# Mixing and transposing softmax heads with two 64x128 TensorE tiles in place of four 64x64 tiles

## The chip, the cores and the metric

The kernel runs on one core of a Trainium2 chip. A core has five engines with instruction streams of their own: TensorE (PE, matrix multiply, results to PSUM), VectorE (DVE), ScalarE (ACT), GpSimd (POOL) and SyncE (SP, which starts DMAs here). The profile shows TensorE in two rows: PE for the matmuls, PEld for the loads of their stationary operand ("weight loads"), which can run beside matmuls. The metric is the device time of one execution in microseconds (us); lower is better. All data is 32-bit floating point.

TensorE multiplies a stationary operand, held in an array of 128 rows by 128 columns, by a moving operand that is streamed past it. A matmul smaller than the array can be put on a part of it, a tile; where its operands lie in the partitions of SBUF and its result in those of PSUM says which tile. A 64x64 tile takes 64 rows (the summed dimension) and 64 columns (the partitions of the result), and four of them fill the array. A 64x128 tile takes 64 rows and all columns, and two fill the array.

## The reference

Four sequences of 2048 tokens with 256 features run through a layer of attention with 16 heads of width 16, whose heads are mixed before and after the softmax, and then through a soft mixture of experts. Both have a residual sum and a layer norm. What matters here is the attention:

```python
logits = jnp.einsum('bhid,bhjd->bhij', q, k) * SCALE
logits = jnp.einsum('bhij,gh->bgij', logits, Wpre)
attn = jax.nn.softmax(logits, axis=-1)
attn = jnp.einsum('bhij,gh->bgij', attn, Wpost)
out = jnp.einsum('bhij,bhjd->bhid', attn, v)
```

For every query i and key j there are 16 scores, which are mixed across heads by Wpre, put through a softmax over keys, mixed across heads by Wpost, and used to weight the values.

## The kernel before

Per sequence, three stages follow one another: `qkv` (projections, rotary embedding, transposes), `attention`, and `moe`. The attention takes over nine tenths of the time. It works on pairs of query blocks: a block is 8 queries with 16 heads, which together fill 128 partitions, and a pair n has two blocks x = 0, 1. A sequence has 128 pairs, all four have 512. The 2048 keys are split into two halves j of 1024 (`HALF`).

For each pair and each half of the keys these steps are run, by functions inside `attention`:

- `raw_bank` (matmul L368, copy L375): scores of the 16 queries and heads for 512 keys, four banks k per half, each on four 128x32 tiles. VectorE or ScalarE copies each bank from PSUM to SBUF as `raw`.
- `logits` (L389): mixing by Wpre, on 64x64 tiles, into PSUM tiles `l` of pool `ps_l`.
- `top` (L402, VectorE): the negated maximum of each row. `expo` (L410, ScalarE): the exponential, to SBUF as `e`, with row sums.
- `weights` (L421 to L432, mostly GpSimd): once per pair, the block matrix `w` in which Wpost is multiplied by the softmax's factors.
- `mix` (matmul L461, copy L470): the changed step. It multiplies by Wpost and transposes at the same time: the stationary operand is a piece of `e` (64 rows of queries and heads, some keys as columns), the moving operand is the matching 64 rows of `w` (64 columns: 16 mixed heads by 4 queries). The result has keys on its partitions, as the next step needs it.
- `values` (L485): the product with v, twice per two pairs, on four 128x32 tiles, 64 columns each.

A call of `mix` is for one block x and one half j. It takes two PSUM tiles `pts[r]`, one for the upper and one for the lower 64 partitions of `e`, each with eight key tiles a (`HT`) of 128 keys. For each a and each r it issued two matmuls, c = 0 and 1, of 64 keys each. So a call has 8 x 2 x 2 = 32 matmuls, and each is recorded in the trace as two weight loads and two matmul instructions, as is every 32-bit matmul here that is not a transpose: 64 of each per call, 128 per two calls, and 131072 in all. Then each `pts[r]` is copied to `aT` by VectorE (V) or ScalarE (S_).

The PSUM tiles of `raw_bank`, `mix` and `values` all come from pool `ps_t`, which has four buffers (L72). A call of `mix` holds two of them until its copies are done; so two calls in a row hold all four, and the raw bank after them starts when the first copy has given one back.

The loop over n is a software pipeline: scores of pair n+1, logits and exponentials of pair n, mixing of pair n-1, values of earlier pairs. On PE the order in a pair, as the trace has it, is: logits of the first half, four raw banks, `mix` of block 0 for both halves (first burst, 128 instructions); logits of the second half, `mix` of block 1 for both halves (second burst, 128 instructions), four raw banks, values. In the source the second half's calls stand so:

```python
if prv:
    mix(n - 1, 1, 0, (S_, S_))
if cur:
    top(n, j, 0)
    expo(n, j, 0)
if prv:
    mix(n - 1, 1, 1, (V, S_))
```

The framework orders the instructions of each engine, so an engine's order may differ from the source's: in the trace, ScalarE runs this exponential before the two copies of the call that stands ahead of it.

Of the kernel before, what the change touches and what calls it, by code (L numbers as in the profile page):

```python
# [16 lines left out]
P = 128  # L17
# [8 lines left out]
def kernel(  # L26
# [20 lines left out]
    nc = tc.nc  # L47
# [36 lines left out]
    for r in range(P // HC):  # L84
        c, i = divmod(r % (KC * IQ), IQ)
# [248 lines left out]
    def attention(b, y, qT, kT, v):  # L334
# [107 lines left out]
        def mix(n, x, j, engs):  # L442

            s = state[n]
            grp, k = divmod(2 * n + x, NB)
            if k == 0 and j == 0:
                aT[grp] = work.tile([P, NT, HEADS, GI], F32, tag="aT", name=f"aT_{b}_{grp}")  # L450
            pts = [
                ps_t.tile([P, HT, HEADS * IQ], F32, tag="t", name=f"t_{b}_{n}_{x}_{j}_{r}")
                for r in range(2)
            ]
            e = s["e", x, j]
            for a in range(HT):
                for r in range(2):
                    rows = slice(64 * r, 64 * (r + 1))
                    for c in range(2):
                        k0 = a * P + 64 * c  # L460
                        nc.tensor.matmul(  # L461
                            pts[r][64 * c : 64 * (c + 1), a, :],
                            e[rows, k0 : k0 + 64],
                            s["w"][rows, 2 * x + j, :],
                            start=True,
                            stop=True,
                        )
            for r in range(2):
                i0 = k * IB + r * IQ
                engs[r](  # L470
                    aT[grp][:, ts(j, HT), :, i0 : i0 + IQ],
                    pts[r].rearrange("p a (g i) -> p a g i", i=IQ),
                )
# [47 lines left out]
        for n in range(n_pairs + 3):  # L521
# [4 lines left out]
            for j in range(2):  # L526
# [4 lines left out]
                if j == 0:  # L531
# [15 lines left out]
                    if prv:  # L547
                        mix(n - 1, 0, 0, (V, S_))
                        mix(n - 1, 0, 1, (V, S_))
                else:  # L550
                    if prv:
                        mix(n - 1, 1, 0, (S_, S_))
# [207 lines left out]
```

## Time and profile before

| | us |
|---|---|
| median of 3 runs | 10240.56 (10240.32 to 10242.80) |
| the profiled execution | 10242.24 |
| its span, first to last instruction | 10240.5 |
| PE busy, all matmuls | 9268.5 |
| PE busy with raw scores (L368) | 3739.1 |
| PE busy with mixing (L461) | 2183.9 |
| PE busy with logits (L389) | 2070.1 |
| PE busy with values (L485) | 1018.0 |
| copies of mixed tiles (L470), ACT and DVE | 1450.4 and 1058.2 |

Busy time of PE counts a moment once, however many tiles work in it, so several matmuls side by side are no longer than one. In a group's line, the first figure after the bar is busy time in us and the second the mean duration of one instruction in ns; that mean is from issue to last result and is far longer than the spacing of instructions, since they overlap. "128*32", "64*64" and so on before the shapes are the rows and columns of the array that an instruction uses. The mean granted clock of TensorE over the execution is 0.986 of the full one; in the attention stage it is 1.00.

### The profile page before, as it was taken

The numbers are of one execution on the slowest core, as the hardware profiler recorded it, in microseconds if no ns is written. First come the engines' busy times: TensorE is split into PE (matmuls) and PEld (weight loads), VectorE is DVE, ScalarE is ACT, GpSimd is POOL, SyncE is SP. The second block draws the span as 40 slices with busy tenths as digits, with TensorE's granted clock in tenths as the row PEclk, the third lists the DMA queues.
The fourth block names the chain that finished last, engine by engine and source line by source line (L and its number), as shares of the span: only waits on it lengthen the run. The fifth ranks groups of instructions, "written<-read, shape, count | busy, mean of one in ns | idle before, by whom it ended". The sixth has DMA issues, their size and how long they took to land.

```text
span 10240.5 us, 523545 instructions
## 1 busy us (share of the span) xinstructions
PE 9268.5 (91%) x248404; PEld 5008.8 (49%) x248404; DVE 5613.3 (55%) x9064; ACT 4995.1 (49%) x9766; POOL 1284.9 (13%) x3409
## 2 busy tenths in 40 slices
PE   8999999997899999999689999999968999999996
PEld 4445545444444445445444545444544444444454
DVE  5555555554555555555455555555545555555554
ACT  3555555553455555555345555555534555555553
POOL 2111111111211111111121111111112111111111
PEclk9999999998999999999899999999989999999998
DMA  0000000000000000000000000000000000000000
GB/s 23 5 5 5 4 5 5 5 4 17 19 5 5 5 4 5 5 5 4 17 19 5 5 5 4 5 5 5 4 17 18 5 5 5 4 5 5 4 4 18
DMA packets 63584, 74.04 MB, mean 7 GB/s; under 512 B 30080, under 2 KB 59904, under 8 KB 61440
## 3 DMA queue, kind: packets, MB, share of 16 engines
q8 instruction: 1946, 31.88, 1.3%
q1 hardware_dynamic: 26880, 25.18, 0.8%
q10 hardware_dynamic: 34560, 15.36, 0.6%
q14 instruction: 198, 1.62, 0.1%
HBM read 32.13 MB, written 8.39 MB: 4 GB/s over the span
## 4 chain that ended last, share of the span: by engine, by line
PE 80%; ACT 9%; DVE 8%; issue 2%; POOL 1%; ACTq 0%; DMA 0%; POOLq 0%; DVEq 0%
PE s L368 36%; PE l L389 19%; PE t L461 10%; PE o L485 9%; DVE m L402 6%; ACT e L410 5%; ACT aT L470 3%; PE pqk L289 1%; PE pz L509 1%; PE pf L680 1%; PE l_d L197 1%; PE o_d L236 1%; POOL xn L591 0%; PE pv L294 0%; POOL xn L592 0%
## 5 line engine op out<-in xcount | busy, mean ns | idle before, releaser
L368 PE MATMUL s<-kT,qb 128*32 128x512 f32 x32768 | 3739.1, 596 | 551.4 <-ACT aT L470 551.3
L402 DVE TENSOR_REDUCE m<-l 128x1 f32<-128x1024 f32 x2048 | 2412.7, 1220 | 1269.8 <-PE l L389 1269.8
L410 ACT ACTIVATE e<-l,m 128x1024 f32<-128x1024 f32 x2048 | 2285.8, 1121 | 1262.7 <-DVE m L402 1262.6
L375 ACT COPY raw<-s 128x512 f32<-128x512 f32 x2048 | 1211.7, 592 | 2809.0 <-PE s L368 2808.4
L461 PEld LDWEIGHTS t<-w,e 64*64 64x64 f32 x131072 | 2103.4, 135 | 754.0 <-issue 685.9
L368 PEld LDWEIGHTS s<-kT,qb 128*32 128x32 f32 x32768 | 966.7, 109 | 2886.8 <-issue 1797.2
L461 PE MATMUL t<-w,e 64*64 64x64 f32 x131072 | 2183.9, 219 | 43.0 <-issue 34.9
L389 PE MATMUL l<-raw,wmix_sb 64*64 64x512 f32 x16384 | 2070.1, 596 | 7.2 <-ACT e L410 3.6
L470 ACT COPY aT<-t 128x512 f32<-128x512 f32 x2560 | 1450.4, 589 | 396.2 <-PE t L461 395.8
L375 DVE COPY raw<-s 128x512 f32<-128x512 f32 x2048 | 1354.7, 681 | 350.3 <-PE s L368 349.6
L470 DVE COPY aT<-t 128x512 f32<-128x512 f32 x1536 | 1058.2, 689 | 338.2 <-PE t L461 338.0
L485 PEld LDWEIGHTS o<-aT,v 128*32 128x32 f32 x65536 | 997.0, 110 | 329.3 <-issue 176.8
L485 PE MATMUL o<-aT,v 128*32 128x64 f32 x65536 | 1018.0, 220 | 31.6 <-issue 26.5
L423 POOL TENSOR_TENSOR f<-m,m 128x4 f32<-128x4 f32 x512 | 101.6, 198 | 6568.8 <-DVE m L421 6568.8
L389 PEld LDWEIGHTS l<-raw,wmix_sb 64*64 64x64 f32 x16384 | 566.5, 133 | 679.6 <-issue 616.8
L429 DVE RECIPROCAL z<-z 128x2 f32<-128x2 f32 x512 | 85.1, 166 | 1081.5 <-POOL z L428 1081.5
L496 DVE COPY aoT<-o 128x32 f32<-128x32 f32 x512 | 98.1, 192 | 1005.9 <-PE o L485 1005.7
L410 ACT ACTIVATION_READ_ACCUMULATOR e<-l,m 128x1 f32 x2048 | 421.9, 206 | 0.0
L343 POOL TENSOR_TENSOR qb<-qT,hmask 128x256 f32<-128x256 f32 x512 | 313.6, 634 | 73.3 <-PE s L368 73.3
L432 POOL TENSOR_TENSOR w<-wblk_sb,f 128x256 f32<-128x256 f32 x512 | 313.7, 613 | 40.3 <-POOL f L430 0.5
L426 POOL TENSOR_TENSOR zf<-f,z 128x4 f32<-128x4 f32 x512 | 102.5, 200 | 987.2 <-ACT f L424 987.2
L315 POOL TENSOR_TENSOR s<-qk,wq 128x256 f32<-128x256 f32 x128 | 115.9, 924 | 478.4 <-DVE qk L299 478.4
(123 smaller groups left out, 2602.0 us busy)
## 6 DMA issues: line engine op xcount, KB each, us to landing
x<-in_x_dram SPq DMA_DIRECT2D x64, 128.0 KB
xr<-in_x_dram SPq DMA_DIRECT2D x64, 128.0 KB
out_dram<-y SPq DMA_DIRECT2D x16, 512.0 KB
wm<-in_w_dram ACTq DMA_DIRECT2D x8, 512.0 KB
wm<-in_w_dram ACTq DMA_DIRECT2D x4, 1024.0 KB
wq<-in_wqkvT_dram ACTq DMA_DIRECT2D x4, 768.0 KB
wq<-in_bqkv_dram ACTq DMA_DIRECT2D x4, 384.0 KB
wq<-in_rope_dram ACTq DMA_DIRECT2D x4, 256.0 KB
```

What stands on the lines that cost most here:

```text
L315: nc.gpsimd.tensor_mul(s[:, :, a, :], qk[:, :, 1 - a, :], ss[a])
L343: nc.gpsimd.tensor_tensor(qb, qT[:, :, ts(n, 2 * IB)].unsqueeze(3).to_broadcast([P, KC, 2 * IB, HC]), hmask.unsqueeze(1).unsqueeze(1).to_b ...
L368: nc.tensor.matmul(pr[32 * c : 32 * (c + 1), :], qb[:, c % 2, i0 : i0 + IQ, :].rearrange("p i h -> p (i h)"), kT[:, c % 2, j0 : j0 + 512], ...
L375: eng(raws[n][j, u][:, ts(jj, 512)], pr)
L389: nc.tensor.matmul(pls[x][64 * u : 64 * (u + 1), n0 : n0 + 512], wmix_sb[64 * x : 64 * (x + 1), :], raws[n][j, u][64 * x : 64 * (x + 1), n ...
L402: nc.vector.tensor_reduce(s["m2"][:, x, j : j + 1], s["l", j][x], AX.X, ALU.max, negate=True)
L410: nc.scalar.activation(e, s["l", j][x], AF.Exp, bias=s["m2"][:, x, j : j + 1], accum_out=s["z2"][:, x, j : j + 1],)
L426: nc.gpsimd.tensor_tensor(zf, f, z2, ALU.mult)
L432: nc.gpsimd.tensor_tensor(w, wblk_sb.rearrange("p g i -> p (g i)").unsqueeze(1).to_broadcast([P, 4, HEADS * IQ]), f.rearrange("p x j -> p ...
L461: nc.tensor.matmul(pts[r][64 * c : 64 * (c + 1), a, :], e[rows, k0 : k0 + 64], s["w"][rows, 2 * x + j, :], start=True, stop=True,)
L470: engs[r](aT[grp][:, ts(j, HT), :, i0 : i0 + IQ], pts[r].rearrange("p a (g i) -> p a g i", i=IQ),)
L485: nc.tensor.matmul(po[32 * c : 32 * (c + 1)].rearrange("p a i -> p (a i)"), v[:, t, g0 * HD : (g0 + 2) * HD], at[:, t, g0 : g0 + 2, :].rea ...
```

## The change

Inside `mix`, the loop over the two halves c of a key tile is gone. One matmul takes all 128 keys of a key tile as columns of its stationary operand, and writes all 128 partitions of the PSUM tile. A call has 16 matmuls on two 64x128 tiles of the array (upper and lower rows), in place of 32 on four 64x64 tiles. What is multiplied, the moving operand, the PSUM tiles and the copies out of them stay as they were.

```diff
             for a in range(HT):
                 for r in range(2):
                     rows = slice(64 * r, 64 * (r + 1))
-                    for c in range(2):
-                        k0 = a * P + 64 * c
-                        nc.tensor.matmul(
-                            pts[r][64 * c : 64 * (c + 1), a, :],
-                            e[rows, k0 : k0 + 64],
-                            s["w"][rows, 2 * x + j, :],
-                            start=True,
-                            stop=True,
-                        )
+                    nc.tensor.matmul(
+                        pts[r][:, a, :],
+                        e[rows, ts(a, P)],
+                        s["w"][rows, 2 * x + j, :],
+                        start=True,
+                        stop=True,
+                    )
```

## The prediction

> **What bounds the kernel now.** I read the page's busy shares first, then the chain that ended last, then the waits, then the timeline of one pair of query blocks in mid-kernel.
>
> ```profile
> PE 9268.5 (91%) x248404; PEld 5008.8 (49%) x248404; DVE 5613.3 (55%) x9064; ACT 4995.1 (49%) x9766; POOL 1284.9 (13%) x3409
> ...
> PE 80%; ACT 9%; DVE 8%; issue 2%; POOL 1%; ACTq 0%; DMA 0%; POOLq 0%; DVEq 0%
> ...
> L461 PEld LDWEIGHTS t<-w,e 64*64 64x64 f32 x131072 | 2103.4, 135 | 754.0 <-issue 685.9
> L368 PEld LDWEIGHTS s<-kT,qb 128*32 128x32 f32 x32768 | 966.7, 109 | 2886.8 <-issue 1797.2
> L461 PE MATMUL t<-w,e 64*64 64x64 f32 x131072 | 2183.9, 219 | 43.0 <-issue 34.9
> ```
>
> TensorE is the bound: busy 91% of the span, 80% of the chain. The mixing matmul (L461) is 2184 us of it. Of the rest, one wait matters, shown by the waits of PE (us in total, times, longest):
>
> ```profile
> PE s L368 <- ACT aT L470: 551.3, 492, 1.5
> ```
>
> Once in nearly each of the 512 pairs, the next raw-score bank waits until ScalarE has copied a mixed tile out of PSUM. The timeline of PE, and then that of ACT, show where:
>
> ```profile
> 4012.73 2.10 PE L461 MATMUL t<-w,e 64*64 64x64 f32 x128
> 4014.64 1.90 PE L389 MATMUL l<-raw,wmix_sb 64*64 64x512 f32 x16
> 4016.36 2.04 PE L461 MATMUL t<-w,e 64*64 64x64 f32 x128
> 4019.64 0.64 PE L368 MATMUL s<-kT,qb 128*32 128x512 f32 x4 [1.24 <-ACT aT L470]
> ```
>
> ```profile
> 4017.91 1.11 ACT L410 ACTIVATE e<-l,m 128x1024 f32<-128x1024 f32 x1 [2.41 <-DVE m L402]
> 4018.92 0.19 ACT L410 ACTIVATION_READ_ACCUMULATOR e<-l,m 128x1 f32 x1
> 4019.02 1.06 ACT L470 COPY aT<-t 128x512 f32<-128x512 f32 x2
> 4019.96 1.14 ACT L410 ACTIVATE e<-l,m 128x1024 f32<-128x1024 f32 x1
> ...
> 4021.15 0.60 ACT L470 COPY aT<-t 128x512 f32<-128x512 f32 x1
> ```
>
> Each pair has two bursts of 128 mix instructions (two calls of mix; one matmul shows as two instructions in this trace: 64 matmuls, 128 rows). Start to start, the first burst takes 4014.64 - 4012.73 = 1.91 us and the logits follow at once. The second has 4019.64 - 4016.36 = 3.28 us until the next work starts, so 1.37 us of it is waiting. ACT sets that end: it runs the exponential, which needs DVE's maximum over the new logits, ahead of the two copies.
>
> Last, what a weight load costs by its width. Weight loads of L461 and of the only stream here whose loads are wide and whose matmuls are short (L627: 128 weight columns, 32 moving columns):
>
> ```profile
> 4012.90 1.21 PEld L461 LDWEIGHTS t<-w,e 64*64 64x64 f32 x76
> ```
>
> ```profile
> 2516.92 1.20 PEld L627 LDWEIGHTS ph<-siT,wm 128*128 128x128 f32 x10
> ```
>
> Less the last load's own duration (135 and, by its tile's rows, 192 ns): 76 loads are 19 rounds of four tiles, 18 steps in 1.21 - 0.135 us less about 20 ns of stagger within a round: 58.5 ns a round. L627 makes 9 steps in 1.20 - 0.192: 112 ns a load. Mean load durations go the same way: 110 ns at 32 columns, 135 at 64, 190 at 128 (o_d, L236), so 0.78 to 0.86 ns per column.
>
> **The change part by part.**
>
> *Removed and added.* A call issues 16 matmuls (32 instructions) in place of 32 (64). Each still streams 64 columns of w; each now loads 128 columns of e, not 64. Per burst there were 128/4 = 32 rounds on four tiles; there will be 64/2 = 32 rounds on two. The count of rounds stays. Each round's stream stays too: 64 columns, about 54 ns if 256 columns take 0.216 us (o_d: eight in 1.89 us, the last 0.38 long). Only the load grows.
>
> *Price of a round.* Before, load (about 53 ns for 64 columns by the 0.78 to 0.86 above) and stream (54) lie beside each other in the same tile: a round takes 58.5 ns, not 107. So a round costs the longer of the two plus some 5 ns. Afterwards the longer is the 128-column load, and L627 measures that directly: 112 ns. No row shows two 64-row loads over the same 128 columns at once; the nearest is L461 itself, whose upper and lower 64-row tiles over the same 64 columns share a 58.5 ns round. So the two loads should overlap. Bounds: 56 ns from below (the round of the values, L485, should both column halves of a load go side by side), 224 from above (two loads one after the other). I take 112; close around it lie 108.5 and 113.5 (58.5 plus 64 columns at 0.78 or 0.86).
>
> *First burst.* 32 x (112 - 58.5) = 1.71 us more, all on the path: PE goes straight on to the logits before and after. 512 x 1.71 = 876 us.
>
> *Second burst.* It becomes 1.91 + 1.71 = 3.62 us, against 3.28 us until the buffer is free today. The wait of 1.37 us vanishes; what is left is 0.34 us, 512 x 0.34 = 174 us, plus 1.37 us for each of the 20 pairs that show no such wait, 27 us. Late next: the buffers of the second call. Its DVE copy could start at 4016.36 + 3.62 + about 0.1 and end near 4020.8; its ACT copy stays behind the second exponential, ending at 4021.75. The four raw banks start 0.87 us apart from 4019.98, the third at 4021.7 and the fourth at 4022.6: both find their buffer free. No new wait.
>
> *The rest at nothing.* The copies (L470) have the same count and shape and run on engines 55% and 49% busy; a later copy is hidden unless PE waits for its buffer, just dealt with. Per first burst, the copies of call one end while call two runs. POOL's weights are due a pair later. No DMA moves, and no queue of SP or POOL is passed. Halving the instruction count is priced at nothing: rounds set the pace, not single instructions, since four of them start within some 20 ns and the next four come 58.5 ns later.
>
> *Sum.* 876 + 174 + 27 = 1077 us. The profiled execution took 10242.2 us (span 10240.5 plus 1.7), the median of the three is 10240.6. 10242 + 1077 = 11319, said as 11320.
>
> *Two rules against the rows.* The Trainium skill, page "TensorE: Matmul & The Clock Gate", Part 3, The mechanism, says that a weight load overlaps running matmuls only where their row groups differ. With two tiles that cover all rows, this speaks for more harm than I forecast; by it a round would be 112 + 54 = 166 ns and the time about 13,090 us. The trace disagrees already: L461 has 53 + 54 ns in 58.5 in the same row groups. The same page, Part 1, on 56 against 53.3 ns, gives a floor of about 25 ns between starts of matmuls, which would make 128 instructions last 3.2 us and their halving a gain; they last 1.91 us, so the floor does not hold across tiles here.
>
> **The rivals.**
>
> *Load and stream one after the other* (166 ns): 32 x 107.5 = 3.44 us a burst; 512 x (3.44 + 3.44 - 1.37) + 27 = 2848, 13,090 us. Against it: the 58.5 ns round. *The two loads one after the other* (224 ns): 5.30 a burst, 512 x 9.23 + 27 = 4750, 14,990 us. Against it: four loads per round today.
>
> *Not slower: the wide load costs no more than two narrow ones.* If a 128-column load of a 64-row tile fills both halves side by side, the round stays at 58.5 ns and the time at 10,242 us; at the pace of the values (L485: 128 in 1.79 us of the chain, 56 ns for four) it gives 32 x 2.5 ns on the first burst alone, since the second waits anyway: 512 x 0.08 = 41, 10,201 us. It decides below 59.7 ns a round (1.2 ns x 32 x 512 = 20 us). For it: L226 has 128-column loads of 141 ns, but as transposes; against: L236 and L627 at 190.
>
> *The wait stays.* Instruction order on ACT isn't the source's (the exponential runs ahead of copies that the source lists first), so it may be laid out anew. If the freeing copy again comes 1.37 us after the burst, 512 x 2 x 1.71 = 1751, 11,990 us. It needs ACT's copy to end after 4021.4; it ends at 4019.6 today.
>
> *The clock falls.* Windows of all engines, with PEclk the third figure from the end:
>
> ```profile
> 2516.40:2518.40 2.00, 2.00 (x18) 2.00 (x19) 0.00 (x0) 1.27 (x1) 0.00 (x0) 0.99 0.00 0
> 2518.40:2521.60 3.20, 3.20 (x16) 3.07 (x15) 0.00 (x0) 0.00 (x0) 0.00 (x0) 0.50 0.00 0
> 2528.60:2579.80 51.20, 36.65 (x163) 27.65 (x162) 27.02 (x89) 12.63 (x41) 0.00 (x0) 1.00 0.01 3
> ```
>
> In the L627 stream PE is always busy by the profile, yet streams only 27 of 112 ns (24%), and the granted clock halves after 2 us. The combine stage streams 16 x (8 x 0.216 + 2 x 0.108) = 31 of 51.2 us (61%) and keeps 1.00. The new bursts stream 54 of 112 (48%) with full work around them: nearer the second. If each burst lost its clock after 2 us, 1.6 us would double: 1024 x 1.6 = 1640 more, 12,960 us.
>
> **How the numbers follow.** Forecast 0.74 (its own range 11,205 to 11,430: at 108.5 ns, 819 + 118 + 27; at 113.5 ns, 901 + 200 + 27 and a first load uncovered by 55 ns in each of 1024 bursts, 56); wait stays 0.06; clock 0.05; load and stream in turn 0.05; loads in turn 0.03; same 0.04; faster 0.03. A measurement here tells 0.2% (20 us) from no change. Slower: 0.74 + 0.06 + 0.05 + 0.05 + 0.03 = 0.93. The range takes the forecast and the wait that stays, 0.80 together: 11,200 to 12,010.
>
> **What would show it.** Right: L461 with 65536 instructions, loads of about 190 ns; 112 ns between loads of one tile; first burst 3.6 us from start to start; the wait of L368 for L470 near nothing; the granted clock in the attention stretch at 1.00. Wrong: L461 loads of 135 ns (not slower), rounds near 166 or 224, a wait of some 500 us kept, or a clock under 1.00 in mid-attention.

## The result, and the profile after

The changed kernel takes 11,420.8 us (median of 4 runs, 11,413.9 to 11,427.9) against 10,241.7 us before (4 runs, 10,240.3 to 10,243.8): a ratio of 1.1151, 95% interval 1.1132 to 1.1170. It is 1179 us slower; the sum of the forecast was 1077. The profiled execution took 11,417.6 us, its span 11,415.9.

Busy shares, chain and the group of the mixing matmul, from the page (the change moves L461 to L459 and L485 to L483):

```profile
PE 11054.1 (97%) x182868; PEld 6671.8 (58%) x182868; DVE 5757.9 (50%) x9064; ACT 5054.9 (44%) x9766; POOL 1290.8 (11%) x3409
...
PE 96%; DVE 2%; POOL 1%; ACT 1%; issue 0%; ACTq 0%; DMA 0%; POOLq 0%; DVEq 0%
...
L459 PEld LDWEIGHTS t<-w,e 64*128 64x128 f32 x65536 | 3748.1, 188 | 844.3 <-issue 782.9
L459 PE MATMUL t<-w,e 64*128 64x64 f32 x65536 | 3889.1, 274 | 5.4 <-POOL w L432 5.4
L368 PE MATMUL s<-kT,qb 128*32 128x512 f32 x32768 | 3736.1, 596 | 0.0
```

Half the instructions take 1.8 times as long. PE now fills the chain, and the raw scores (L368) wait for nothing, where they had waited 551 us for ScalarE's copies.

Weight loads of one microsecond, then PE over a pair (start, duration, group, count):

```profile
4401.41 1.20 PEld L459 LDWEIGHTS t<-w,e 64*128 64x128 f32 x20
```

```profile
4415.63 3.79 PE L459 MATMUL t<-w,e 64*128 64x64 f32 x64
4419.35 1.95 PE L389 MATMUL l<-raw,wmix_sb 64*64 64x512 f32 x16
4421.23 3.79 PE L459 MATMUL t<-w,e 64*128 64x64 f32 x64
4424.95 0.64 PE L368 MATMUL s<-kT,qb 128*32 128x512 f32 x4
```

Twenty loads are ten rounds of two tiles. Less the last load's 188 ns and the 7 ns between the two of a round, nine steps take 1.005 us: 112 ns a round, as the forecast had taken from the stream of L627. The first burst lasts 4419.35 - 4415.63 = 3.72 us from start to start (1.91 before, 3.62 forecast), the second 4424.95 - 4421.23 = 3.72 (3.28 before with its wait, 3.62 forecast). The logits between them, which the forecast had left alone, went from 4016.36 - 4014.64 = 1.72 us to 4421.23 - 4419.35 = 1.88.

The clock stayed. Two stretches inside the attention stages (the third figure from the end is the granted clock):

```profile
98.00:2698.00 2600.00, 2598.65 (x44606) 1553.72 (x44598) 1313.50 (x1955) 1210.20 (x2300) 263.87 (x775) 1.00 0.01 3
2953.00:5560.00 2607.00, 2604.38 (x44932) 1562.81 (x44932) 1314.02 (x1958) 1211.78 (x2302) 263.88 (x775) 1.00 0.01 3
```

**Where the time came from.** The span grew by 11,415.9 - 10,240.5 = 1175.4 us, and this can be booked in full on PE:

| | before | after | difference |
|---|---|---|---|
| PE busy with mixing | 2183.9 | 3889.1 | +1705.2 |
| PE busy with anything else while no mixing runs | 7084.6 | 7165.0 | +80.4 |
| PE idle, L368 waiting for L470 | 551.3 | 0 | -551.3 |
| PE idle, "issue" (nothing in the profile released it) | 63.5 | 17.2 | -46.3 |
| PE idle, the rest | 357.2 | 344.6 | -12.6 |

The 80.4 us are not work of another line: L368, L389 and L485 each have as much busy time as before or a little less. They are overlap lost. Matmuls of neighbouring steps run into each other at their ends, and such a moment is booked under mixing: 231.6 us before, 142.5 after. Mixing shares 124 us less with the logits on both sides of them, and 35 us more with the raw banks, which now follow the second burst at once.

### The profile page after: what moved, and what is told of

It reads as the page before. It is cut to its first block, busy times and chain, and to the rows that moved or that the text cites. A ratio compares the mean times of both kernels' runs of the same rounds, so it can differ in the third digit from the quotient of the medians.

```text
span 11415.9 us, 392473 instructions
## 1 busy us (share of the span) xinstructions
PE 11054.1 (97%) x182868; PEld 6671.8 (58%) x182868; DVE 5757.9 (50%) x9064; ACT 5054.9 (44%) x9766; POOL 1290.8 (11%) x3409
## 4 chain that ended last, share of the span: by engine, by line
PE 96%; DVE 2%; POOL 1%; ACT 1%; issue 0%; ACTq 0%; DMA 0%; POOLq 0%; DVEq 0%
PE t L459 33%; PE s L368 32%; PE l L389 17%; PE o L483 8%; PE pqk L289 1%; PE pz L507 1%; PE pf L678 1%; PE l_d L197 1%; PE o_d L236 1%; PE pv L294 0%; POOL xn L589 0%; POOL xn L590 0%; DVE y L256 0%; PE pr L322 0%; DVE y L681 0%
## 5 line engine op out<-in xcount | busy, mean ns | idle before, releaser
L459 PEld LDWEIGHTS t<-w,e 64*128 64x128 f32 x65536 | 3748.1, 188 | 844.3 <-issue 782.9
L459 PE MATMUL t<-w,e 64*128 64x64 f32 x65536 | 3889.1, 274 | 5.4 <-POOL w L432 5.4
L368 PE MATMUL s<-kT,qb 128*32 128x512 f32 x32768 | 3736.1, 596 | 0.0
L368 PEld LDWEIGHTS s<-kT,qb 128*32 128x32 f32 x32768 | 961.6, 110 | 2299.6 <-issue 2111.8
L389 PE MATMUL l<-raw,wmix_sb 64*64 64x512 f32 x16384 | 2068.5, 602 | 0.0
L375 DVE COPY raw<-s 128x512 f32<-128x512 f32 x2048 | 1411.1, 689 | 774.4 <-PE s L368 774.4
L483 PEld LDWEIGHTS o<-aT,v 128*32 128x32 f32 x65536 | 994.0, 110 | 315.9 <-issue 315.3
L483 PE MATMUL o<-aT,v 128*32 128x64 f32 x65536 | 1014.1, 220 | 17.2 <-issue 17.2
L389 PEld LDWEIGHTS l<-raw,wmix_sb 64*64 64x64 f32 x16384 | 541.6, 132 | 702.0 <-issue 616.9
L605 PE MATMUL pu<-ident,u 128*128 128x128 f32 x128 | 23.4, 342 | 157.1 <-DVE u L600 157.1
```

What stands on the lines that cost most here:

```text
L368: nc.tensor.matmul(pr[32 * c : 32 * (c + 1), :], qb[:, c % 2, i0 : i0 + IQ, :].rearrange("p i h -> p (i h)"), kT[:, c % 2, j0 : j0 + 512], ...
L375: eng(raws[n][j, u][:, ts(jj, 512)], pr)
L389: nc.tensor.matmul(pls[x][64 * u : 64 * (u + 1), n0 : n0 + 512], wmix_sb[64 * x : 64 * (x + 1), :], raws[n][j, u][64 * x : 64 * (x + 1), n ...
L459: nc.tensor.matmul(pts[r][:, a, :], e[rows, ts(a, P)], s["w"][rows, 2 * x + j, :], start=True, stop=True,)
L483: nc.tensor.matmul(po[32 * c : 32 * (c + 1)].rearrange("p a i -> p (a i)"), v[:, t, g0 * HD : (g0 + 2) * HD], at[:, t, g0 : g0 + 2, :].rea ...
```

## Experiments

**Theory.** A round of tiles costs the longer of its weight load and its stream; at 128 columns the load is the longer, 107 of 112 ns. The wait for PSUM buffers in the second burst hides part of it. After the result, one more term: at a change of tile shape (64x64 to 64x128 and back) the next loads cannot be fetched beside the running matmuls. **Rivals:** load and stream in turn; two tiles are slow in themselves, whatever the width of a load; the wait hid nothing.

### One burst at a time

Edit of `wide_first`; `wide_second` has `x == 1`:

```diff
-                    for c in range(2):
...
+                    if x == 0:
+                        nc.tensor.matmul(
+                            pts[r][:, a, :],
+                            e[rows, ts(a, P)],
...
+                    else:
+                        for c in range(2):
...
```

> Only the first burst of each pair (block x = 0) runs on two 64x128 tiles; the second keeps four 64x64 tiles. Theory 'load pace plus a late first load' (a round is set by the 128-column load at 112 ns, and at a change of tile shape the next loads can't be fetched ahead, about 0.15 us at the end of a wide burst): the first burst goes from 1.92 to 3.72 us from start to start, all of it on the path, 512 x 1.80 = 922 us more, about 11,165; the wait of L368 for L470 stays at some 500 us. Theory 'load pace alone': 512 x 1.71 = 876 more, about 11,117. If the wait hid a part here too, it would be under 10,900.

> Only the second burst (block x = 1) runs on two 64x128 tiles. Theory 'load pace plus a late first load': the burst goes from 3.28 us (of it 1.37 waiting) to 3.72, and the logits ahead of it from 1.72 to 1.88 because the first loads of the burst are no longer fetched beside the logits: 512 x (0.44 + 0.16) = 305 more, about 10,545, or some 50 less where the kernel before had further waits that go too; the wait of L368 for L470 goes to near nothing. Theory 'load pace alone': 0.34 a pair, about 10,440. Without any hiding in the wait it would be 512 x 1.96 = 1000 more.

Measured: `wide_first` 11,158.4 us, ratio 1.0888 (1.0872 to 1.0905), close to the 11,165 of the theory with the late load; `wide_second` 10,493.6, ratio 1.0240 (1.0225 to 1.0256), each against 10,249.3 on the same chip: 909 and 244 us. Their sum, 1153, is close to the whole change's 1179: the parts add up. The waits of `wide_first` on PE:

```profile
PE s L368 <- ACT aT L479: 625.9, 504, 1.5
```

PE of `wide_first`, then of `wide_second`:

```profile
4408.15 3.79 PE L460 MATMUL t<-w,e 64*128 64x64 f32 x64
4411.87 1.95 PE L389 MATMUL l<-raw,wmix_sb 64*64 64x512 f32 x16
4413.64 2.04 PE L470 MATMUL t<-w,e 64*64 64x64 f32 x128
4416.92 3.64 PE L368 MATMUL s<-kT,qb 128*32 128x512 f32 x32 [1.24 <-ACT aT L479]
```

```profile
4405.20 2.10 PE L470 MATMUL t<-w,e 64*64 64x64 f32 x128
4407.12 1.90 PE L389 MATMUL l<-raw,wmix_sb 64*64 64x512 f32 x16
4408.94 3.79 PE L460 MATMUL t<-w,e 64*128 64x64 f32 x64
4412.66 3.64 PE L368 MATMUL s<-kT,qb 128*32 128x512 f32 x32
```

The wide first burst costs its full price while the wait in the second stays (626 us). The wide second burst has no wait behind it. Both say what the logits between the bursts pay at a change of shape: 1.72 us with 64x64 on both sides (before), 4413.64 - 4411.87 = 1.77 behind a wide burst, 4408.94 - 4407.12 = 1.82 ahead of one, 1.88 with wide on both sides. `wide_second` came 51 us under the 10,545 expected from steady pairs, as its expectation had allowed for further waits that go.

The weight loads show why the logits' price depends on their neighbour. The first loads of the second burst, before and then after:

```profile
4015.93 0.15 PEld L461 LDWEIGHTS t<-w,e 64*64 64x64 f32 x4 [0.28 <-issue]
```

```profile
4421.23 0.41 PEld L459 LDWEIGHTS t<-w,e 64*128 64x128 f32 x6 [0.81 <-issue]
```

With the same shape on both sides, four loads come 0.43 us ahead of the burst's first matmul (4016.36), beside the logits. With different shapes the first load starts together with the first matmul (4421.23).

### Twice the stream

Edit of `wide_stream2`, on the changed kernel; `narrow_stream2` has the same moving operand and `a : a + m` on the four tiles of before:

```diff
+                    m = min(2, HT - a)
                     nc.tensor.matmul(
-                        pts[r][:, a, :],
+                        pts[r][:, a : a + m, :],
                         e[rows, ts(a, P)],
-                        s["w"][rows, 2 * x + j, :],
+                        s["w"][rows, 2 * x + j, :].unsqueeze(1).to_broadcast([64, m, HEADS * IQ]),
```

> The changed kernel, but each mixing matmul streams its 64 columns twice (128 columns into two neighbouring key tiles of the PSUM bank; the next matmul overwrites the second copy; the last key tile has one). Loads as in the changed kernel. Theory 'the load sets the round, the stream lies beside it': stream 108 ns against load 107, so the round stays at 112 to 115 ns and the time at 11,420 to 11,500. Theory 'load and stream in turn': 54 ns more in 28 of 32 rounds of each burst, 1024 x 28 x 0.054 = 1550 more, about 12,970.

> The kernel before on four 64x64 tiles, each mixing matmul streaming its 64 columns twice, as in the run wide_stream2. Loads stay 64 columns wide. Theory 'a round is the longer of load and stream': the stream of 108 ns now sets the round at 112 ns, as the 128-column load does in the changed kernel, but the tiles keep the shape of the logits, so the first loads of a burst are still fetched ahead. 28 of 32 rounds grow by 54 ns: 1.51 us on the first burst, 1.51 - 1.37 = 0.14 on the second: 512 x 1.65 + 27 = 872 more, about 11,110. Theory 'load and stream in turn': the same 54 ns a round, so the time is alike, but it can't explain the 58.5 ns of now. Theory 'a stream of 128 columns costs no more than one of 64 (a fixed cost for each instruction)': 10,241.

Measured: 11,711.3 us, ratio 1.1428 (1.1409 to 1.1448), and 11,542.7, ratio 1.1267 (1.1251 to 1.1284). Both are over what the theory expected (11,500 at most, and 11,110). The bursts tell why. PE of `wide_stream2`, then of `narrow_stream2`:

```profile
4403.98 3.79 PE L460 MATMUL t<-w,e 64*128 64x128 f32 x64
4407.70 1.95 PE L389 MATMUL l<-raw,wmix_sb 64*64 64x512 f32 x16
4409.58 3.79 PE L460 MATMUL t<-w,e 64*128 64x128 f32 x64
4413.88 3.64 PE L368 MATMUL s<-kT,qb 128*32 128x512 f32 x32 [0.51 <-ACT aT L469]
```

```profile
4401.26 3.52 PE L462 MATMUL t<-w,e 64*64 64x128 f32 x128
4404.60 1.90 PE L389 MATMUL l<-raw,wmix_sb 64*64 64x512 f32 x16
4406.32 3.47 PE L462 MATMUL t<-w,e 64*64 64x128 f32 x128
4410.82 3.64 PE L368 MATMUL s<-kT,qb 128*32 128x512 f32 x32 [1.04 <-ACT aT L471]
```

On two wide tiles, twice the stream costs the first burst nothing: 4407.70 - 4403.98 = 3.72 us, as with 64 columns. A 128-column load and a 128-column stream lie beside each other in the same rows and columns. That rules out load and stream in turn, and leaves the load as what sets the pace of the changed kernel. The load is also seen to be that long: at the start of a burst, where loads run ahead, the first two of a tile start 108 ns apart, against 55 ns before. A fixed cost of the wide shape that has nothing to do with its load is not tested: every 128-column matmul here has a load of its own. On four narrow tiles the same stream does cost: 4404.60 - 4401.26 = 3.34 us against 1.91. So a round is the longer of the two, from either side. And the logits of `narrow_stream2` still take 4406.32 - 4404.60 = 1.72 us: it is the tile shape that costs the 0.16 us, not a slow burst as such.

The excess of both runs is in the second burst, where the wait came back, 262 us in `wide_stream2` and 526 in `narrow_stream2`. ScalarE of `narrow_stream2` shows how (that of `wide_stream2` has the same order of these copies and exponentials):

```profile
4407.87 1.11 ACT L410 ACTIVATE e<-l,m 128x1024 f32<-128x1024 f32 x1 [2.41 <-DVE m L402]
4408.88 0.19 ACT L410 ACTIVATION_READ_ACCUMULATOR e<-l,m 128x1 f32 x1
4409.00 1.11 ACT L410 ACTIVATE e<-l,m 128x1024 f32<-128x1024 f32 x1
4410.01 0.19 ACT L410 ACTIVATION_READ_ACCUMULATOR e<-l,m 128x1 f32 x1
4410.10 0.19 ACT L424 ACTIVATE f<-f 128x4 f32<-128x4 f32 x1
4410.20 1.55 ACT L471 COPY aT<-t 128x512 f32<-128x512 f32 x3
```

Both exponentials now stand ahead of the copies that free the buffers; before, one did. The order on ScalarE was laid out anew, which is the rival "the wait stays" of the prediction, with its mechanism, in another kernel than the one it was stated for.

### Two tiles with narrow loads

```diff
-            for a in range(HT):
-                for r in range(2):
-                    rows = slice(64 * r, 64 * (r + 1))
-                    for c in range(2):
+            for c in range(2):
+                for a in range(HT):
+                    for r in range(2):
+                        rows = slice(64 * r, 64 * (r + 1))
```

> The kernel before, with the matmuls of a call in another order: first all with keys 0 to 63 of a key tile, then all with keys 64 to 127, so that only two 64x64 tiles of the array (upper and lower rows, same columns) alternate at a time. Loads are 64 columns wide, as before; the shape of the tiles is that of the logits. Theory 'the pace is that of a tile': 64 rounds of 58.5 ns a burst, 3.78 us, 512 x (1.86 + 0.50) = 1208 more at most, 11,400 to 11,450, close to the changed kernel but by twice the rounds at half the length, and with the logits ahead of the second burst still at 1.72 us. Theory 'four loads or matmuls may be under way wherever they are': no change, 10,241.

Measured: 11,106.3 us, ratio 1.0837 (1.0820 to 1.0853): between the two theories, nearer to the first. The start of a burst, weight loads:

```profile
4408.99 0.84 PEld L461 LDWEIGHTS t<-w,e 64*64 64x64 f32 x26 [0.84 <-issue]
```

Thirteen rounds of two: twelve steps in 0.84 - 0.135 us, 59 ns each. Two tiles with 64-column loads keep the round of four tiles; two tiles alone do not make it 112 ns, so the width of the load does. The burst is shorter than 64 such rounds, though: 3.3 us with two logits matmuls in it, in place of 3.78. The start times have 55 rounds in place of 64: at each of the three changes of column half in a burst, three rounds have four starts in place of two. I read this as matmuls of the other column half that begin while the first half still has rounds to go, tiles that are free running ahead of busy ones; the trace doesn't name a matmul's tile, so this isn't shown.

### Filling the wait, and taking it away

First, `values` moved ahead, so that PE has other work while ScalarE is late:

```diff
                 else:
+                    if val:
+                        values(grp, hf)
                     if prv:
                         mix(n - 1, 1, 0, (S_, S_))
...
-                    if val:
-                        values(grp, hf)
```

> The kernel before, with the call of values moved from the end of the second half of a pair to ahead of the first mix of block 1. PE then has 1.9 us of other work while DVE takes the maximum and ACT the exponential, so the copies that free the PSUM buffers should be done when the raw banks come. Theory 'the wait of L368 for L470 is a wait for the buffer, and can be filled': 551 to 700 us less, 9,540 to 9,690. If ACT puts the second exponential ahead of the copies, some 0.8 us of the wait stays, up to 9,950. Theory 'the wait only moves' (to the second call of mix, which needs the same buffers): 10,240.

> The changed kernel with values moved as in the run values_early. There is no wait left for the longer second burst to use up. Theory 'the wait hid 1.37 us per pair of the change': the step from values_early to this one is 512 x (1.80 + 1.80 + 0.16) = 1925 us, against 1179 between the two kernels of the case; in time some 11,420 again, since PE works without a pause in both. If the change cost the same 1179 here, the wait hid nothing.

Measured: `values_early` 10,529.4 us, ratio 1.0277 (1.0261 to 1.0292), and `values_early_wide` 11,438.5, ratio 1.1167 (1.1149 to 1.1186). The expected gain was a loss. PE of `values_early`:

```profile
4416.31 1.99 PE L485 MATMUL o<-aT,v 128*32 128x64 f32 x128
4418.23 0.32 PE L461 MATMUL t<-w,e 64*64 64x64 f32 x3
4419.26 2.08 PE L461 MATMUL t<-w,e 64*64 64x64 f32 x125 [0.70 <-issue]
4421.27 1.04 PE L368 MATMUL s<-kT,qb 128*32 128x512 f32 x3
4423.16 1.06 PE L368 MATMUL s<-kT,qb 128*32 128x512 f32 x8 [0.85 <-issue]
```

The waits of PE in `values_early`:

```profile
PE t L461 <- issue: 525.3, 445, 1.8
PE s L368 <- ACT aT L470: 11.8, 10, 1.5
```

The wait of L368 for ScalarE's copies could be filled: it fell from 551 to 12 us. But PE now stops in the middle of a step, mostly in the mix, for some 1.1 us in nearly each pair, and nothing that the profile names released it. This is not the rival's wait for a buffer: the stop stands at another matmul from pair to pair (after 3 of the burst in the pair shown, after 83 in another), and mostly the matmul that ends it waits for no semaphore.

The stops follow the count of instructions. Of the 489 steps from one stop to the next (over 0.5 us each), 486 are within three of a multiple of 128 matmuls. With as many weight loads, 128 matmuls are 256 instructions, and that is what one packet of the instruction queue holds (q8 on the page: 1946 packets of 16 KB for 498,146 instructions of PE and its loads). By the trace's DMA records, 483 of the 490 stops end 1.2 to 1.7 us after such a packet has ended; only 9% of arbitrary moments lie there. In the rows above, packets end at 4417.79 and 4421.78, and PE goes on at 4419.26 and 4423.16. So the stops look like waits for instructions: values and mix side by side issue 512 instructions in some 3.8 us, and no two packets start less than 3.2 us apart. No run changes the supply of instructions alone.

With its stop the second burst is hardly shorter than it was with the wait, or longer (3.04 us in the pair shown, 3.55 in another, 3.28 before). The logits, now ahead of values of another tile shape, take 4416.31 - 4414.48 = 1.83 us in place of 1.72. The step to `values_early_wide` was 909 us and not 1925, since `values_early` had got these stops in place of its wait; this pair does not test how much the wait hid.

So the order of ScalarE itself was set, first for the two copies of the first call (`copies_first`):

```diff
             for r in range(2):
                 i0 = k * IB + r * IQ
-                engs[r](
+                s["copied", r] = engs[r](
...
                     if cur:
                         top(n, j, 0)
-                        expo(n, j, 0)
+                        if prv:
+                            with tc.issue_after(state[n - 1]["copied", 1].ins):
+                                expo(n, j, 0)
+                        else:
+                            expo(n, j, 0)
```

then also for the copy of the second call (`copies_first2`), and this on the changed kernel too (`copies_first2_wide`):

```diff
                         mix(n - 1, 1, 1, (V, S_))
+                        last = state[n - 1]["copied", 1].ins
                         state.pop(n - 1)
                     if cur:
                         top(n, j, 1)
-                        expo(n, j, 1)
+                        if prv:
+                            with tc.issue_after(last):
+                                expo(n, j, 1)
+                        else:
+                            expo(n, j, 1)
```

> The kernel before, with ScalarE's order in the second half of a pair set by hand: the two copies of mix(n-1, 1, 0) stand ahead of the first exponential, as the source lists them (in the trace of before they stand behind it). No other edit. The copies can run when their tiles are mixed, about 1 us after the burst begins, so the first raw bank need not wait for the exponential. Theory 'the wait of L368 for L470 is an order of ScalarE over four PSUM buffers': most of the 551 us goes; the fourth raw bank may still wait some 0.5 us for the copy of the second call, which stands behind both exponentials: 9,540 to 9,850. Theory 'the wait only moves', as it did in the run values_early: 10,240 or more.

> As copies_first, and the copy of mix(n-1, 1, 1) on ScalarE stands ahead of the second exponential too, so all four buffers are free when the raw banks want them. Theory 'an order of ScalarE over four buffers': no wait of L368 for L470 is left, 512 x 1.37 = 700 us less at most, 9,540 to 9,650. If the later exponentials now hold up the next logits, up to 10,240.

> The changed kernel with the order of ScalarE as in copies_first2. There PE works without a pause already, so the order should gain nothing: about 11,400 to 11,440. The step from copies_first2 to this one is then the whole price of the wide tiles, with no wait to use up: 512 x (1.80 + 1.80 + 0.16) = 1925 us less whatever wait copies_first2 keeps; theory 'the wait hid nothing of the change' gives 1180.

Measured, against 10,231.9 us of the kernel before on the same chip: `copies_first` 9,830.8, ratio 0.9609 (0.9594 to 0.9623); `copies_first2` 9,764.3, ratio 0.9545 (0.9531 to 0.9559); `copies_first2_wide` 11,434.4, ratio 1.1177 (1.1158 to 1.1195). PE of `copies_first2`:

```profile
4409.85 2.04 PE L461 MATMUL t<-w,e 64*64 64x64 f32 x128
4411.83 3.90 PE L368 MATMUL s<-kT,qb 128*32 128x512 f32 x32
4415.54 1.97 PE L485 MATMUL o<-aT,v 128*32 128x64 f32 x128
```

The raw banks follow the second burst at once: 4411.83 - 4409.85 = 1.98 us where it was 3.28. They then take 4415.54 - 4411.83 = 3.71 us, against 3.46 without a wait in them (`wide_second`), so 0.25 us are left: the third bank starts at 4413.80, just after ScalarE's third copy, which runs from 4413.15 to 4413.74 behind an exponential. `copies_first2` beats both kernels of the case, by 4.5% and some 14.5%, on the four narrow tiles. It came 114 us above the upper end of the 9,540 to 9,650 expected; `copies_first` was within its 9,540 to 9,850.

With the order set by hand, the step from narrow to wide tiles costs 11,434.4 - 9,764.3 = 1670 us, where it cost 1179 in the case. What the kernel before waited for had hidden at least some 490 us of the change. The expected 1925 was too much: it counted 3.76 us a pair, while steady pairs of the two traces differ by 20.12 - 16.67 = 3.45. `copies_first2` still has 0.25 us of wait in such a pair, its second burst takes 1.98 us where 1.92 was counted, and many of its pairs are longer than 16.67, with 66 us of "issue" idle in the whole run.

## Why the prediction was right

- **A round of 112 ns:** right to the nanosecond, from a stream of another stage whose loads have the same width. That two 64-row loads run at once, which no row of before showed, holds.
- **The longer of load and stream:** right; `wide_stream2` and `narrow_stream2` show it from both sides. The rivals "in turn" fall.
- **The wait of L368 goes to nothing:** right, and so is "no new wait": the third and fourth raw banks found their buffers. The rival "the wait stays" did not happen here; with doubled streams it did.
- **The clock holds at 48% streaming:** right.
- **First burst 1.71 us:** under by 0.10 (3.72 against 3.62). The step took the old burst's length and added 32 times the growth of a round, and so kept the old ends. At a wide burst's end the logits' loads can't be fetched ahead.
- **Logits between the bursts, priced at nothing:** wrong by 0.16 us a pair. The prediction passed over that logits and mix share the 64x64 shape before, and that only afterwards they differ.
- **Second burst, 0.34 us left of its growth:** it was 0.44 (3.72 against 3.28), by the same 0.10 as in the first burst. The 1.37 us hidden in a pair were right: the burst itself grew by 3.72 - 1.91 = 1.81 us, and 0.44 of it showed.
- **1.37 us more in each of 20 pairs that show no wait, 27 us:** this did not come. No pair grew by clearly more than the 2.40 us of a steady one.
- **Half the instructions, priced at nothing:** PE's "issue" idle went from 63.5 to 17.2 us, a gain of 46 (the last section has what these stops follow).
- **The sum:** a steady pair grew by 20.12 - 17.72 = 2.40 us, not 2.05, which would be 1229 us in 512 pairs. So the terms that were too small (0.35 us a pair) left out 179 us, and the 27 that did not come and the 46 of "issue" made up for part of it: 1077 + 179 - 27 - 46 = 1183, where 1179 was measured. That the sum is nearer than the terms is luck; the round of 112 ns and the hidden wait are not.

## What to carry to other kernels

A wider stationary operand here halved the instructions but not the work: with few moving columns, price a TensorE tile shape by the longer of its weight load (per column of the stationary operand) and its stream, per round of tiles that run at once. Check which neighbours share the tile shape, because here loads were fetched ahead across a boundary where it stayed the same, and not where it changed. And when a longer step costs less than its own growth, look for the wait that it used up: that wait was free time, and here an explicit order of three copies on ScalarE, on the old tile shape, made 4.5% out of it.

## What the runs showed of the hardware that was not expected

- A change of tile shape has a price at both ends: 0.05 us for logits behind a wide burst, 0.10 ahead of one, and about 0.1 more at the end of the burst.
- PE's "issue" stops follow the instruction queue. In the twelve traces, 678 of the 685 such stops over 0.5 us end 1.2 to 1.7 us after the end of a 16 KB packet of that queue, where 6 to 10% of arbitrary moments lie. The kernel before has 34 of them, 49 us, with 1946 packets; the changed kernel 6, 17 us, with 1434. `narrow_stream2` has as many packets as before but spreads its instructions over longer bursts: 12 stops, 25 us. This fits a PE that at times runs out of instructions where short ones stand close; no run changed the supply alone.
- Tiles of one column half seem to run ahead of the other half by some three rounds of 58 ns (`narrow_two`); no run was made for it.
